# Three of 313 row gathers replaced by single-row copies on SyncE through a table in DRAM

## The chip, the cores and the metric

The kernel runs on one core of one Trainium2 chip. The metric is the time of one execution on the device in microseconds (us). The engines are called as in the profile: PE (TensorE, matrix products; PEld its weight loads), DVE (VectorE), ACT (ScalarE), POOL (GpSimd) and SP (SyncE, which computes nothing here and issues DMAs in the order of its program).

## The reference

One block of a graph network (PaiNN), a residual sum and a layer norm. There are 1250 nodes with 512 features (384 of a vector part `v`, 128 of a scalar part `s`) and 40000 edges, sorted by target node.

```python
x_j = x[src]                                   # a row of its source node for each edge
v_j, s_j = x_j[:, :384].reshape(E, 128, 3), x_j[:, 384:]
s_j = silu(s_j @ W1 + b1) @ W3 + b3            # depends on the node alone
split = s_j * (rbf(edge_weight) * cutoff @ W2 + b2)
s1, s2, s3 = split[:, :128], split[:, 128:256], split[:, 256:]
v_msg = v_j * s1[:, :, None] + s3[:, :, None] * edge_attr[:, None, :]
x = x + segment_sum(concat([v_msg, s2]), dst)
...                                            # second half: messages that depend on the source node alone
return layernorm(x_in + x)
```

## The kernel before, in words

What depends on a node alone is computed once for each node and written to a table in DRAM, `table1`, with rows of 640 numbers (2560 bytes). In the main loop each edge needs the row of its source node, times factors of its own, summed over the edges of a target.

The edges are cut into 79 chunks of 512 and these into tiles of 128 edges, one edge to a partition. Four chunks make a group, and a batch is four tiles, one of each chunk of the group. There are 80 batches (`NT`), numbered `t`: 76 full ones and four with two or three tiles, 313 tiles in all. The loop is written out, so every engine has a straight list of instructions, in the order in which the code makes them.

In step `t` of the loop:

- `messages(t)`: DVE multiplies the gathered rows by the edge factors `eb` in place (L938 and L940), then makes `hot`, `spread` and `pair`, small tables that say which target an edge has.
- `add_messages(t - 1)`: PE sums the messages of the batch before by target (L974, L980).
- `edge_factors(t + 1)`: PE makes `eb` for the next batch (L928); its last instruction is kept in the name `made`.
- `gather(t + 3)`: POOL fetches the rows of the batch three ahead, one indirect DMA for each tile (L769); the first of a batch also waits for `made`. A batch goes into the next of five rooms of SBUF, three of the tile `more` and two of `nodes`.
- other work at steps given by tables (`first`, `early`, `mid`, `late`, `dve`), which for each block of 128 nodes makes the second half's rows and starts the last products.

SP does the small transfers of that work. `fetch_part` (L1088) brings a block of `x` in four quarters into `node_x`, one quarter a step, behind `made`; `take_block` on DVE (L1106) reads it one step after the last quarter for the first block, three steps after it for the others. `keep_part` (L1099) copies the sum of `x` and the first half to `resid` in DRAM, also in quarters and behind `made`. `store_begun` (L1405) writes partial products to `spilled`. Each DMA that SP issues waits for the one eight before it on SP, since eight semaphores are used in turn.

Of the kernel before, what the change touches and what calls it, by code (L numbers as in the profile page):

```python
# [11 lines left out]
F32 = mybir.dt.float32  # L12
# [3 lines left out]
I32 = mybir.dt.int32  # L16
# [5 lines left out]
P = 128  # L22
C = 128
V = 3 * C
# [11 lines left out]
CHUNK = 512  # L36
TPC = CHUNK // P
CPG = 4
SHARE = 16
MARGIN = 8  # L40
# [10 lines left out]
GROUP = 4  # L51
LEAD = 3
LAG = 2


def by_component(ap):
# [8 lines left out]
def gnn_resnorm(  # L65
# [350 lines left out]
    with tc.If(misses_v == 0):  # L416
        windowed(tc, sh)
# [201 lines left out]
def windowed(tc, sh):  # L619
# [13 lines left out]
    nc = tc.nc  # L633
# [12 lines left out]
    def lanes(g, i, j):  # L646

        c = g * CPG + j
        if c >= NCH:
            return 0  # L650
        n = CHUNK if c < NCH - 1 else last_rows
        return max(0, min(P, n - i * P))


    batches = [(g, i) for g in range(NGR) for i in range(TPC) if lanes(g, i, 0)]
    NT = len(batches)

    def tiles(g, i):
        return [j for j in range(CPG) if lanes(g, i, j)]
# [15 lines left out]
        return max(i for i in range(TPC) if lanes(g, i, j))  # L675

    resid = tc.dram_tile([NP, width], F32, name="resid")
    spilled = tc.dram_tile([(NB + 2) * P, width], F32, name="spilled")
    counts = sh.counts
    by_group = counts.rearrange("s (p h) n -> s h p n", h=2)  # L680
# [2 lines left out]
    with tc.tile_pool(  # L683
        name="msg", bufs=4
# [78 lines left out]
        def gather(t, behind=None):  # L763

            g, i = batches[t]
            rows_t = next(rooms)
            for j in tiles(g, i):
                n = lanes(g, i, j)
                got = nc.gpsimd.indirect_dma_start(  # L769
                    out=rows_t[:n, j, :],  # L770
                    out_offset=None,
                    in_=sh.table1,
                    in_offset=bass.IndirectOffsetOnAxis(
                        ap=sh.src_i[:n, g, i * CPG + j : i * CPG + j + 1], axis=0
                    ),
                )
                if behind is not None and j == 0:
                    tc.add_manual_dep(
                        got.ins, behind.ins.name, sync,
                        reason="so that rows come while PE is ahead of DVE",  # L780
                    )
            clear_rest(t, rows_t, nc.gpsimd)
            rows_of[t] = rows_t


        def make_turns(g, n, part):
# [60 lines left out]
        def clear_rest(t, tile, engine=nc.vector):  # L847
            g, i = batches[t]
            for j in tiles(g, i):
                m = lanes(g, i, j)  # L850
                if m < P:
                    engine.memset(tile[m:, j], 0.0)
# [58 lines left out]
        def new_banks(name, sizes):  # L911

            factor_banks.close()
            banks.push(factor_banks)
            of = factor_banks.enter_context(tc.tile_pool(name=name, bufs=1, space=PSUM))
            return [
                of.tile([P, n, BANK], F32, name=f"{name}_{k}") for k, n in enumerate(sizes)
            ]
# [5 lines left out]
        def edge_factors(t):  # L924
            g, i = batches[t]
            for j in tiles(g, i):
                rows = slice(j * FEAT, j * FEAT + N_RBF + 1 + CARRY)
                made = nc.tensor.matmul(  # L928
                    made_in[t][:, j, : V + CARRY], turned[g][rows, i, :], sh.w2_sb[rows, :],
                    start=True, stop=True,  # L930
                )
            return made

        def messages(t):
            g, i = batches[t]
            msg = rows_of.pop(t)
            for js, n, m in runs(g, i):
                nc.vector.tensor_mul(msg[:m, js, V:], msg[:m, js, V:], factors_of(t, js)[:m, :, C:V])  # L938
            for js, n, m in runs(g, i):
                nc.vector.tensor_mul(  # L940
                    msg[:m, js, :V].rearrange("p t (k c) -> p t k c", k=3),
                    msg[:m, js, :V].rearrange("p t (k c) -> p t k c", k=3),
                    factors_of(t, js)[:m, :, None, :C].to_broadcast([m, n, 3, C]),
                )
            make_hot(t)
            make_spread(t)
            run(amid, t)
            make_pair(t)
            msgs[t] = msg
# [18 lines left out]
        def add_messages(t):  # L968
            g, i = batches[t]
            if i == 0:  # L970
                aggs[g] = ps_sum.tile([P, width], F32, name="agg")
            agg, msg, js = aggs[g], msgs.pop(t), tiles(g, i)
            for j in js:
                nc.tensor.matmul(  # L974
                    agg[j * WIN : (j + 1) * WIN, :], hots[t][:, j, :],
                    msg[:, j, :width], start=(i == 0), stop=False, skip_group_check=True,
                )
            for c in range(3):
                for j in js:
                    nc.tensor.matmul(  # L980
                        agg[j * WIN : (j + 1) * WIN, c * C : (c + 1) * C],
                        spread[t][:, j, c, :], msg[:, j, width:],
                        start=False, stop=(i == last_tile(g, j) and c == 2),
                        skip_group_check=True,
                    )

        def count_links(t):

            g, i = batches[t]
            if i == 0:  # L990
                adjs[g] = all_links
            adj, one, pair, js = adjs[g], onehots.pop(t), pairs.pop(t), tiles(g, i)
            to = adj[:, : PARTS * REACH].rearrange("s (p n) -> s p n", n=REACH)
            if i == 0 and g:
                nc.tensor.matmul(
                    to[:, :, : REACH - GSPAN], ident, passed.pop(g),
                    start=True, stop=False, skip_group_check=True,
                )
            for j in js:
                m = lanes(g, i, j)  # L1000
                at = j * SHARE

                nc.tensor.matmul(  # L1003
                    to[:, :, at : at + WIN], one[:m, j, :],
                    pair[:m, j, :].rearrange("e (p n) -> e p n", n=WIN),
                    start=(i == 0 and j == js[0] and g == 0), stop=(i == last_tile(g, j)),
                    skip_group_check=True,
                )
# [457 lines left out]
        first, early, late, dve, mid, amid = {}, {}, {}, {}, {}, {}  # L1466

        def at(when, step, rank, fn, *args):
            when.setdefault(step, []).append((rank, fn, args))
# [16 lines left out]
        for g in range(1, NGR, 2):  # L1486
            base, n = 4 * g - 4, min(2, NGR - g)
# [169 lines left out]
        def run(when, step):  # L1657
            for _, fn, args in sorted(when.get(step, []), key=lambda task: task[0]):
                fn(*args)
# [63 lines left out]
        at(dve, 4, 9, sh.part_bias, nc.vector, node_x[:, : 2 * C], slice(V, V + 2 * C))  # L1723
        at(dve, 4, 9.1, nc.vector.memset, node_x[:MARGIN, : 2 * C], 0.0)
        ahead = 3
        for t in range(ahead - 1):
            gather(t)
        gather(ahead - 1, edge_factors(0))
        behind = set(amid) - {last + 1 for last in last_step.values()}
        for t in range(max(*first, *early, *late, *dve, *mid) + 1):  # L1730
            if t < NT:
                messages(t)
            if t == NT - 4:
                assert all(len(tiles(*batches[u])) == CPG // 2 for u in range(NT - 3, NT))
                made_in[NT - 3], made_in[NT - 2] = new_banks("halves", [CPG // 2] * 2)
                made_in[NT - 1] = made_in[NT - 3]
            if t == NT - 1:
                out_banks.update(zip(in_factors, new_banks("out", [1] * CPG), strict=True))
            run(first, t)
            if 1 <= t <= NT:  # L1740
                add_messages(t - 1)
                if t not in behind:
                    count_links(t - 1)
            run(early, t)
            if t + 1 < NT - 2:
                made = edge_factors(t + 1)
            if t + 1 in (NT - 3, NT - 2):
                edge_factors(t + 2)
            if t + ahead < NT:
                gather(t + ahead, made if t + ahead < NT - 2 else None)  # L1750
            if t in behind:
                count_links(t - 1)
            run(mid, t)
            run(late, t)
            run(dve, t)
        soon_out = 0, 1, 2
        for k, rows in enumerate((upper, lower)):
            for b in soon_out:
# [80 lines left out]
def _general(ctx, tc, sh):  # L1839
# [170 lines left out]
    def edge_sums(table, sums, begin, finish, add, pool, ps_agg):  # L2010
# [13 lines left out]

        for step in range(NT + LAG):
            t = step
            if t < NT:
# [9 lines left out]
                nc.vector.tensor_scalar(hots[t], lane, slots[:, t, 4:5], None, op0=ALU.is_equal)  # L2037
            t = step - LAG
            if t >= 0:
# [134 lines left out]
```

## Time and profile before

| | |
|---|---|
| time, median of 3 runs | 480.09 us (478.63 to 480.22) |
| profiled execution | 480.96 us |
| its span, first to last instruction | 479.2 us |
| busy PE / DVE / ACT / POOL | 84% / 89% / 78% / 70% |
| gathers of L769 | 313, 304.4 us busy, 104.1 us idle ahead of them |
| main loop, first to last L938 of full batches | 35.7 to 420.5 us, some 5.1 us a batch |
| DMA | 123.29 MB, mean 257 GB/s |

Busy shares are means over the whole span. Sequencer work (SP's DMA issues, register instructions, waits) is not counted as busy and has rows of its own, with names that end in q. "Idle before" is time in which an engine stood still ahead of an instruction, and the releaser named is what ended it; "issue" means that nothing in the profile was waited for.

### The profile page before, as it was taken

The numbers are of one execution on the slowest core, as the hardware profiler recorded it, in microseconds if no ns is written. First come the engines' busy times: TensorE is split into PE (matmuls) and PEld (weight loads), VectorE is DVE, ScalarE is ACT, GpSimd is POOL, SyncE is SP. The second block draws the span as 40 slices with busy tenths as digits, with TensorE's granted clock in tenths as the row PEclk, the third lists the DMA queues.
The fourth block names the chain that finished last, engine by engine and source line by source line (L and its number), as shares of the span: only waits on it lengthen the run. The fifth ranks groups of instructions, "written<-read, shape, count | busy, mean of one in ns | idle before, by whom it ended". The sixth has DMA issues, their size and how long they took to land. (4 is left out here: it accounts for less than half of the span.)

```text
span 479.2 us, 11259 instructions
## 1 busy us (share of the span) xinstructions
PE 402.6 (84%) x4259; PEld 229.3 (48%) x4259; DVE 427.8 (89%) x675; ACT 375.3 (78%) x971; POOL 334.9 (70%) x364
## 2 busy tenths in 40 slices
PE   8645586878879778798889888989999999999992
PEld 6322243445445345444435544555555655555782
DVE  6569899999999899999999999999999999978584
ACT  4377846689869968877977897799899889967672
POOL 9267777777777777777777777777777777771530
PEclk9857979899999999989989999999999999999998
DMA  8887888788888888888888988888888888879024
GB/s 238 301 247 253 254 265 271 240 279 262 281 254 272 289 259 275 270 269 255 280 276 255 293 267 280 266 291 287 287 275 293 265 284 291 280 242 319 4 71 151
DMA packets 37810, 123.29 MB, mean 257 GB/s; under 512 B 7124, under 2 KB 9782, under 8 KB 37746
## 3 DMA queue, kind: packets, MB, share of 16 engines
q0 software_dynamic: 25568, 104.34, 69.0%
q1 hardware_dynamic: 10834, 17.35, 10.6%
q10 hardware_dynamic: 1344, 0.79, 0.5%
q8 instruction: 35, 0.57, 0.5%
q14 instruction: 29, 0.24, 0.2%
HBM read 112.94 MB, written 9.51 MB: 256 GB/s over the span
## 5 line engine op out<-in xcount | busy, mean ns | idle before, releaser
L769 POOL DMA_INDIRECT more<-table,src_i x189 | 184.6, 977 | 66.3 <-issue 48.1
L769 POOL DMA_INDIRECT nodes<-table,src_i x124 | 119.8, 966 | 37.8 <-issue 33.2
L903 ACT ACTIVATE one<-one,weight,src_f 128x128 f16<-128x128 f16 x313 | 128.5, 482 | 0.2
L928 PE MATMUL eb<-w_sb,basis_t 25*128 25x388 f32 x614 | 74.1, 551 | 54.3 <-DVE spread L881 43.9
L893 ACT ACTIVATE one<-number,low 128x128 f16<-128x128 f16 x313 | 99.8, 392 | 11.2 <-PE adj L1003 11.2
L940 DVE TENSOR_TENSOR more<-more,eb 128x1536 f32<-128x1536 f32 (+2 forms) x48 | 81.8, 1705 | 0.0
L938 DVE TENSOR_TENSOR more<-more,eb 128x1024 f32<-128x1024 f32 (+2 forms) x48 | 57.0, 1190 | 15.0 <-PE eb L928 8.2
L928 PEld LDWEIGHTS eb<-w_sb,basis_t 25*128 25x128 f32 x614 | 24.7, 187 | 76.5 <-DVE spread L881 63.7
L974 PE MATMUL agg<-more,hot 128*32 128x512 f32 x378 | 52.8, 624 | 0.0
L940 DVE TENSOR_TENSOR nodes<-nodes,eb 128x1536 f32<-128x1536 f32 x30 | 52.4, 1747 | 0.0
L980 PEld LDWEIGHTS agg<-more,spread 128*32 128x32 f32 x1134 | 33.5, 111 | 30.2 <-issue 29.6
L938 DVE TENSOR_TENSOR nodes<-nodes,eb 128x1024 f32<-128x1024 f32 x30 | 36.5, 1216 | 6.9 <-PE eb L928 4.0
L881 DVE TENSOR_TENSOR spread<-hot,eb 128x384 f32<-128x384 f32 (+1 forms) x74 | 40.4, 547 | 2.5
L980 PE MATMUL agg<-more,spread 128*32 128x128 f32 x1134 | 40.2, 273 | 0.0
L958 DVE TENSOR_TENSOR pair<-number,column 128x640 f16<-128x640 f16 (+1 forms) x81 | 38.5, 476 | 0.0
L1003 PE MATMUL adj<-pair,one 128*128 128x160 f16 x313 | 35.4, 235 | 0.3 <-DVE basis L827 0.3
L974 PE MATMUL agg<-nodes,hot 128*32 128x512 f32 x248 | 34.9, 619 | 0.0
L980 PEld LDWEIGHTS agg<-nodes,spread 128*32 128x32 f32 x744 | 22.7, 112 | 20.0 <-issue 19.6
L1003 PEld LDWEIGHTS <-one 128*128 128x128 f16 x313 | 21.6, 100 | 16.0 <-issue 13.5
L845 ACT COPY basis_t<-work 128x512 f32<-128x512 f32 x20 | 11.6, 580 | 22.5 <-PE work L840 22.5
L1378 PE MATMUL begun<-upper,cast 128*128 128x512 f32 x57 | 27.8, 487 | 0.0
L980 PE MATMUL agg<-nodes,spread 128*32 128x128 f32 x744 | 27.5, 277 | 0.0
(299 smaller groups left out, 697.3 us busy)
## 6 DMA issues: line engine op xcount, KB each, us to landing
table<-more SPq DMA_DIRECT2D x10, 320.0 KB
more<-table,src_i POOLq DMA_INDIRECT x189, 4.2
spilled<-begun SPq DMA_DIRECT2D x10, 256.0 KB
more<-spilled SPq DMA_DIRECT2D x2, 1280.0 KB
node_x<-in_x_dram SPq DMA_DIRECT2D x35, 64.0 KB
nodes<-table,src_i POOLq DMA_INDIRECT x124, 4.2
out_dram<-more SPq DMA_DIRECT2D x7, 256.0 KB
nodes<-in_x_dram POOLq DMA_DIRECT2D x2, 768.0 KB
```

What stands on the lines that cost most here:

```text
L769: got = nc.gpsimd.indirect_dma_start(out=rows_t[:n, j, :], out_offset=None, in_=sh.table1, in_offset=bass.IndirectOffsetOnAxis(ap=sh.src_i ...
L881: nc.vector.tensor_mul(spread[t][:m, js], hots[t][:m, js, None, :].to_broadcast(shape), carried(t, js, m)[:, :, :3, None].to_broadcast(shape),
L893: nc.scalar.activation(onehots[t][:, j, :], number[:, :P], AF.Abs, bias=low[:, e : e + 1])
L903: nc.scalar.activation(one, one, AF.Relu, scale=less[:, e : e + 1], bias=worth[:, e : e + 1])
L928: made = nc.tensor.matmul(made_in[t][:, j, : V + CARRY], turned[g][rows, i, :], sh.w2_sb[rows, :], start=True, stop=True,)
L938: nc.vector.tensor_mul(msg[:m, js, V:], msg[:m, js, V:], factors_of(t, js)[:m, :, C:V])
L940: nc.vector.tensor_mul(msg[:m, js, :V].rearrange("p t (k c) -> p t k c", k=3), msg[:m, js, :V].rearrange("p t (k c) -> p t k c", k=3), fac ...
L958: nc.vector.tensor_tensor(pair[:m, js, :].rearrange("p t (l h) -> p t l h", h=2), number[:m, : PARTS * WIN].rearrange("p (l h) -> p l h", ...
L974: nc.tensor.matmul(agg[j * WIN : (j + 1) * WIN, :], hots[t][:, j, :], msg[:, j, :width], start=(i == 0), stop=False, skip_group_check=True,)
L980: nc.tensor.matmul(agg[j * WIN : (j + 1) * WIN, c * C : (c + 1) * C], spread[t][:, j, c, :], msg[:, j, width:], start=False, stop=(i == la ...
L1003: nc.tensor.matmul(to[:, :, at : at + WIN], one[:m, j, :], pair[:m, j, :].rearrange("e (p n) -> e p n", n=WIN), start=(i == 0 and j == js[ ...
L1378: nc.tensor.matmul(acc, casts[a, b], rows[:, a, :], start=(start and a == first and k == 0), stop=(stop and a == end - 1 and k == 1),)
```

## The change

One of the four tiles of the batches 23, 47 and 71 (every 24th full batch, the tile of the last chunk) is no longer gathered. `stage_sources` copies the node numbers of its 128 edges to DRAM before the loop. In 16 portions of eight rows, spread over the steps `t - 23` to `t - 6`, `stage_rows` has SP load node numbers into registers, 16 at a time, and issue one DMA for each edge, from the node's row of `table1` to the edge's row of `stage`, both in DRAM; the row's address comes from the register. In `gather`, three steps ahead of use, one plain DMA of SP brings the 128 rows to the tile's place. All else is as before.

```diff
+STAGE_EVERY = 24
+ROWS_AT_ONCE = 16
...
+    full_batches = [t for t in range(NT) if all(lanes(*batches[t], j) == P for j in range(CPG))]
+    staged = {t: k for k, t in enumerate(full_batches[STAGE_EVERY - 1 :: STAGE_EVERY])}
+    stage = tc.dram_tile([len(staged) * P, V + 2 * C], F32, name="stage")
+    stage_src = tc.dram_tile([len(staged), P], I32, name="stage_src")
...
             for j in tiles(g, i):
                 n = lanes(g, i, j)
+                if t in staged and j == CPG - 1:
+                    continue
                 got = nc.gpsimd.indirect_dma_start(
...
+            if t in staged:
+                k = staged[t]
+                nc.sync.dma_start(rows_t[:, CPG - 1, :], stage[k * P : (k + 1) * P, :])
             clear_rest(t, rows_t, nc.gpsimd)
             rows_of[t] = rows_t
+
+        def stage_sources(t):
+            g, i = batches[t]
+            edge = (g * CPG + CPG - 1) * CHUNK + i * P
+            nc.sync.dma_start(
+                stage_src[staged[t] : staged[t] + 1, :],
+                sh.src[edge : edge + P].rearrange("(o e) -> o e", o=1),
+            )
+
+        def stage_rows(t, first, n):
+            k = staged[t]
+            if first % ROWS_AT_ONCE == 0:
+                _, at_stage[t] = nc.values_load_multi_w_load_instructions(
+                    stage_src[k : k + 1, first : first + ROWS_AT_ONCE],
+                    engines=(mybir.EngineType.SP,), min_val=0, max_val=sh.n_nodes - 1,
+                    skip_runtime_bounds_check_because="nodes of edges lie in the features",
+                )
+            for r in range(first, first + n):
+                nc.sync.dma_start(
+                    stage[k * P + r : k * P + r + 1, :],
+                    sh.table1[bass.ds(at_stage[t][r % ROWS_AT_ONCE] + MARGIN, 1), :],
+                )
...
         ahead = 3
+        to_stage, at_stage = {}, {}
+        for u in staged:
+            stage_sources(u)
+            n = 8
+            for k in range(P // n):
+                to_stage.setdefault(u - STAGE_EVERY + 1 + k * 19 // 16, []).append((u, k * n, n))
...
             run(dve, t)
+            for task in to_stage.get(t, ()):
+                stage_rows(*task)
```

The instruction lists show it at three places. Lines of the changed kernel are numbered anew (L1088, L1099, L1405 and L769 are now L1121, L1132, L1438 and L777; the new ones are L792, L799, L807 and L813). First, SP at the start of the loop, before:

```order
L1719 DMA node_x<-in_L_gnn_bu_dram 3x128 x2
L1088 DMA node_x<-in_x_dram 16x512
L1088 DMA node_x<-in_x_dram 8x512
L1088 DMA node_x<-in_x_dram 32x512 x7
L1099 DMA resid<-h_t 32x512 x4
```

and now, with what each instruction waits for (DMAHW is one of SP's eight semaphores; `ISA` is the register instruction that makes an address):

```order
L1752 DMA node_x<-in_L_gnn_bu_dram 3x128 [waits DMAHW6_49]
L1752 DMA node_x<-in_L_gnn_bu_dram 3x128 [waits DMAHW7_49]
L799 DMA stage_src<-in_src_dram 16x8 [waits DMAHW0_49]
L799 DMA stage_src<-in_src_dram 16x8 [waits DMAHW1_49]
L799 DMA stage_src<-in_src_dram 16x8 [waits DMAHW2_49]
L807 TENSOR_LOAD stage_src [waits DMAHW0_49]
L813 ISA
L813 DMA stage<-table_170 16x40 [waits DMAHW3_49]
```

Between the constants and the first quarter of `node_x` now stand the node numbers' copies and 40 rows, each a register instruction and a DMA that is cut in 16 pieces of 40 numbers.

Second, SP around batch 23, before (the third node block's quarters and the second block's copies to `resid`):

```order
L1088 DMA node_x<-in_x_dram 32x512 [waits DMAHW5_49,DVE_49,PE_49]
L1088 DMA node_x<-in_x_dram 32x512 [waits DMAHW6_49,PE_49]
L1088 DMA node_x<-in_x_dram 32x512 [waits DMAHW7_49,PE_49]
L1088 DMA node_x<-in_x_dram 32x512 [waits DMAHW0_49,PE_49]
L1099 DMA resid<-h_t 32x512 [waits DMAHW1_49,PE_49]
L1099 DMA resid<-h_t 32x512 [waits DMAHW2_49]
L1099 DMA resid<-h_t 32x512 [waits DMAHW3_49,PE_49]
L1099 DMA resid<-h_t 32x512 [waits DMAHW4_49]
```

and now:

```order
L813 DMA stage<-table_170 16x40 [waits DMAHW7_49]
L1121 DMA node_x<-in_x_dram 32x512 [waits DMAHW0_49,DVE_49,PE_49]
L792 DMA nodes<-stage 128x640 [waits DMAHW4_49,DMAHW3_49,DMAHW5_49,DMAHW2_49,DMAHW6_49,DMAHW1_49,DMAHW7_49,DMASW1_49,DMASW0_49]
L1121 DMA node_x<-in_x_dram 32x512 [waits PE_49] x3
L1132 DMA resid<-h_t 32x512 [waits PE_49]
L1132 DMA resid<-h_t 32x512
L1132 DMA resid<-h_t 32x512 [waits PE_49]
L1132 DMA resid<-h_t 32x512 [waits DMAHW0_49]
L807 TENSOR_LOAD stage_src [waits DMAHW1_49]
L813 ISA
```

The load of the staged tile (L792) waits for all rows of it, and the next tile's rows begin behind the four copies to `resid`, which wait for PE.

Third, POOL at the gathers of batch 23, before:

```order
L769 DMA nodes<-table_170,src_i 128x640 [waits DMASW2_49,DVE_49,PE_49]
L769 DMA nodes<-table_170,src_i 128x640 [waits DMASW3_49]
L769 DMA nodes<-table_170,src_i 128x640 [waits DMASW4_49]
L769 DMA nodes<-table_170,src_i 128x640 [waits DMASW5_49]
L769 DMA nodes<-table_170,src_i 128x640 [waits DMASW6_49,DVE_49,PE_49]
```

and now:

```order
L777 DMA nodes<-table_170,src_i 128x640 [waits DMASW2_49,DVE_49,PE_49]
L777 DMA nodes<-table_170,src_i 128x640 [waits DMASW3_49]
L777 DMA nodes<-table_170,src_i 128x640 [waits DMASW4_49]
L777 DMA nodes<-table_170,src_i 128x640 [waits DMASW5_49,DVE_49,PE_49]
L777 DMA nodes<-table_170,src_i 128x640 [waits DMASW6_49]
```

The batch's fourth gather is gone, and the fourth row is now the first gather of batch 24.

## The prediction

> **What bounds the kernel now.** I read the waits of DVE and POOL first, then the busy time by stretches, then SP's own rows. The waits (engine, line, releaser: us in total, times, longest):
>
> ```profile
> POOL more L769 <- issue: 48.1, 158, 0.3
> POOL nodes L769 <- issue: 33.2, 109, 0.3
> DVE more L938 <- PE eb L928: 8.2, 12, 2.7
> DVE more L938 <- DMA more<-table,src_i: 4.1, 5, 1.4
> DVE nodes L938 <- DMA nodes<-table,src_i: 1.1, 1, 1.1
> ```
>
> POOL waits for nothing but its own issue, 0.30 us ahead of each gather, while DVE waits only six times for gathered rows, 5.2 us in all. The stretches (length, then PE, PEld, DVE, ACT, POOL busy with counts, clock, DMA share, GB/s) show why:
>
> ```profile
> 180.00:220.00 40.00, 34.27 (x404) 18.57 (x400) 38.01 (x55) 33.08 (x89) 30.64 (x31) 0.96 0.85 268
> 340.00:380.00 40.00, 38.97 (x433) 21.90 (x432) 38.60 (x57) 36.22 (x95) 30.45 (x32) 1.00 0.88 284
> ```
>
> POOL's 32 gathers with 0.30 us between them fill 40 us: 32 x (0.95 + 0.30) = 40.0. DVE is busy 38.0 to 38.6 of the same 40. So POOL sets the pace by a hair, DVE stands right behind, and a batch takes 5 us on both. The batches that matter here begin with these DVE rows (start, length, and in brackets the idle time and its releaser):
>
> ```profile
> 153.87 1.21 DVE L938 TENSOR_TENSOR nodes<-nodes,eb 128x1024 f32<-128x1024 f32 x1
> 164.97 1.22 DVE L938 TENSOR_TENSOR more<-more,eb 128x1024 f32<-128x1024 f32 x1 [1.43 <-DMA more<-table,src_i]
> 277.81 1.22 DVE L938 TENSOR_TENSOR more<-more,eb 128x1024 f32<-128x1024 f32 x1 [0.38 <-DMA more<-table,src_i]
> 288.83 1.22 DVE L938 TENSOR_TENSOR nodes<-nodes,eb 128x1024 f32<-128x1024 f32 x1 [1.12 <-DMA nodes<-table,src_i]
> 400.44 1.21 DVE L938 TENSOR_TENSOR more<-more,eb 128x1024 f32<-128x1024 f32 x1
> ```
>
> Batches 23, 47 and 71 start at 153.87, 277.81 and 400.44. Those are the deadlines of the three staged tiles.
>
> **What it removes.** Three gathers, 3 x 1.25 = 3.75 us of POOL. Of this DVE can cash only its own waits for gathers. After batch 23 POOL is 1.25 us further ahead: the wait of 1.43 shrinks to 0.18, and later batches and later gathers both move up by 1.25, so their waits stay. After batch 47 another 1.25 us removes the 1.12. After batch 71 no wait for gathers is left to remove. Gain: 1.25 + 1.12 = 2.4 us.
>
> **What it adds on SP.** Per staged tile 128 pairs of a register instruction (`ISA`) and a row DMA, eight loads of 16 registers, and one load of the tile. Nearest rows of SP (first the timeline: start, length; then two lines' own views: ns min/median/max):
>
> ```profile
> 25.23 1.40 SPq L400 DMA_DIRECT2D w_sb<-in_L_gnn_W_dram  x4
> 26.68 0.60 SPq L401 DMA_DIRECT2D w_sb<-in_L_gnn_b_dram  x1
> 27.32 0.44 SPq L153 DMA_DIRECT2D u_sb<-in_L_gnn_U_dram  x1
> 32.46 1.49 SPq L1719 DMA_DIRECT2D node_x<-in_L_gnn_bu_dram  x2
> ...
> L415 SPq TENSOR_LOAD <-missed_i x1: 485/485/485, 31.5 to 31.5; - x1
> L415 SPq FUSED_REGOPS  x1: 192/192/192, 32.0 to 32.0; - x1
> ...
> L1088 SPq DMA_DIRECT2D node_x<-in_x_dram x37: 309/311/382, 67.3 to 400.1; - x37
> ```
>
> The register instruction: L415's has three register operations, and so has each row's (+8, x640, x4). 0.19, with the 0.04 us to the next instruction (26.68 + 0.60 to 27.32) 0.23 us.
>
> The row DMA: between 0.31 (plain loads, L1088) and 0.77 (L1719, 1.49 + 0.04 over 2). The plain ones, L400 among them at (26.68 - 25.23) / 4 = 0.36 with the gap, carry a mark in the built program that L401, L1719 and all 384 row DMAs lack. L401 stands in an unbroken run of DMAs, as the rows will: I take its 0.60 + 0.04 = 0.64. A row is then 0.87 us, 128 rows 111.4.
>
> The load of 16 registers: L415 shows one register from SBUF in 0.485. Lower end 0.485, if 16 come as one. Upper end: 0.192 as the part paid once (the register instruction, which reads no memory) and 0.293 for each register, 4.88. The row is near neither, so I take the middle, 2.68, with the gap 2.72; eight are 21.8. Nothing in the trace reads registers from DRAM, and the upper end could be passed there.
>
> The Trainium skill, Runtime: NRT & Kernel Launch, "Instruction fetch mechanics", gives about 200 ns for each register of such a load even in bulk: 3.2 us for 16 is an estimate by that page, and the sum below would be 593 instead of 581. No run here shows a load of more than one register; its 485 ns fit the page as little as they contradict it.
>
> So a staged tile holds SP for T = 111.4 + 21.8 = 133.2 us, against some 124 us from one deadline to the next.
>
> **What is queued around it on SP.** SP takes its instructions in order, and the old transfers stand between the rows. Today SP mostly waits, and its transfers start when PE and DVE let them:
>
> ```profile
> SPq L1088 <- PE eb L928: 159.1, 35, 6.1
> SPq L1088 <- DVE h_t L1116: 65.5, 8, 11.4
> ...
> 158.59 5.90 SPq L1099 DMA_DIRECT2D resid<-h_t  x4
> ...
> 287.74 0.34 SPq L1405 DMA_DIRECT2D spilled<-begun  x1
> ...
> DMA to landing us min/median/max: 3.8/4.2/5.8
> ```
>
> The last row is that of the gathers, nearest for what a transfer of SP takes to land: 4.2 us. Tile by tile:
>
> Tile 1 can begin once SP is past L1719 (33.95) and the node numbers have landed: 38.2. Then T; 14 old transfers in between, x 0.36 = 5.0; the load of the tile waits for the last rows, 4.2, and lands 4.2 later: 38.2 + 133.2 + 5.0 + 8.4 = 184.8, where DVE wants it at 153.87. Stall 30.9.
>
> Tile 2 stands behind the four L1099, which wait for PE of batches 23 and 24 and end 164.49 - 153.87 = 10.6 after batch 23 starts. 10.6 + 133.2 + 18 x 0.36 + 8.4 = 158.7, against 277.81 - 153.87 = 123.94. Stall 34.8.
>
> Tile 3 stands behind L1405, which ends 288.08 - 277.81 = 10.3 after batch 47 starts. 10.3 + 133.2 + 5.0 + 8.4 = 156.9, against 122.63. Stall 34.3.
>
> Inside these stretches the old transfers are late too: the last quarter of the first node block stands behind 56 rows, four loads and four transfers, 38.2 + 48.7 + 10.9 + 1.4 + 4.2 = 103.4, where DVE first reads it at 87.3:
>
> ```profile
> L1106 DVE TENSOR_TENSOR x<-node_x,work x9: 664/674/700, 87.3 to 414.3; 128x384 f32<-128x384 f32 x9
> ```
>
> DVE thus stops there for 16 us. This is part of the 30.9 and not added to it, since SP is not held up by it. The spills and the copies to `resid` leave late in the same way, also inside the stalls. The gain of 2.4 us goes: where SP sets the start of batches 23, 47 and 71, POOL has been ahead for long.
>
> **DMA engines.**
>
> ```profile
> q0 software_dynamic: 25568, 104.34, 69.0%
> q1 hardware_dynamic: 10834, 17.35, 10.6%
> q10 hardware_dynamic: 1344, 0.79, 0.5%
> ```
>
> Each row is cut in 16 pieces of 160 bytes: 6144 pieces and at most as many closing packets. A packet costs 28 ns (q10: 0.5% x 16 x 479.2 us / 1344) to 75 (q1): 21 to 58 us on each of 16 engines, less 3/313 of 69%. At a share of 0.85 this delays landings somewhat. I put it at nothing, as 4.2 us of landing is covered by the 7 us in which eight rows issue (each row DMA waits for the eighth before it); what is left uncovered, two landings a tile, is in the range.
>
> **Sum.** 30.9 + 34.8 + 34.3 = 100.0 on the profiled execution's 480.96 us (span 479.2; the median of the runs, 480.09, is 0.2% lower): 581 us. In short, time = 481 + 3T - 300, as long as T is above about 102.
>
> **Rivals.**
> *SP keeps up* (the other side). One mechanism: a row with its share of the register loads issues fast enough. Stalls vanish at T = 98 to 102, 0.77 us a row all in, and the first node block is on time at 0.7. With plain DMAs of 0.31 it would be: 128 x 0.58 + 21.8 = 96. Then the gain stands, 478.6 us. Against it: L401, L1719 and the register instruction. 0.16; landings behind fuller DMA engines may eat 2.4 us, so 0.07 for faster, 0.09 for no change.
> *Register loads come as one*, 0.485: T = 111.4 + 8 x 0.525 = 115.6, 481 + 47 = 528. With rows a little cheaper too this reaches down to 490. For it: one instruction; against: 16 registers have to be written. 0.16.
> *Registers come one by one*: T = 111.4 + 8 x 4.92 = 150.8, 634 us. 0.10.
> *Landing paces the rows*: beyond 7 us of landing the wait for the eighth before decides; at 10 us T is 160 + 21.8, 727 us. The gathers' longest is 5.8. 0.02.
>
> **How the numbers follow.** My forecast, each tile late by a fifth to a good third of the 124 us, 550 to 620 us in all, has the remaining 0.56. The range for 8 in 10 takes in the cheap loads and most of the dear ones: 488 to 640. Half a per cent is about what a measurement of this kernel can tell from no change. Faster 0.07, same 0.09, slower 0.84.
>
> **What would show it.** Right: DVE waits of tens of us ahead of L938 at batches 23, 47 and 71, released by the DMA from `stage`, and waits for `node_x` at L1106; SP rows back to back at 0.87 us a pair; register loads of 2 to 4 us; POOL now waiting for PE. Wrong, if the row DMA takes 0.31 or the pair runs under 0.7, if SP idles between rows, or if DVE stops for `node_x` alone; and if row DMAs wait for their eighth predecessor, the landing was the price and not the issue.

## The result, and the profile after

The changed kernel takes 533.76 us (median of 4 runs, 530.62 to 534.63) against 479.51 us before (median of 4, 478.63 to 480.22): ratio 1.112, 95% interval 1.107 to 1.117, 54 us more. The profiled execution took 534.63 us, its span 532.7 against 479.2. Lines of the changed kernel have the new numbers: L777 gathers, L961 makes `eb`, L971 and L973 multiply, L1121 is `fetch_part`, L1132 `keep_part`, L1438 `store_begun`, L1139 reads `node_x`, L1149 writes `h_t`, L792 loads the staged tile, L807 the registers, L813 copies a row.

First the same two stretches as in the prediction, busy time by engine (PE, PEld, DVE, ACT, POOL), clock, DMA share and GB/s, of the changed kernel:

```profile
180.00:220.00 40.00, 33.10 (x407) 18.67 (x408) 38.39 (x56) 34.31 (x93) 30.40 (x32) 0.99 0.87 268
340.00:380.00 40.00, 30.54 (x313) 16.50 (x314) 29.21 (x42) 29.46 (x75) 23.61 (x25) 0.91 0.73 228
```

In the first the loop runs as before (32 gathers, DVE 38.4 of 40), although SP copies the second tile's rows all through it. In the second, 7 gathers and 9 us of DVE are missing: the loss sits in single stops. The waits, as before (us in total, times, longest):

```profile
POOL nodes L777 <- PE eb L961: 33.0, 11, 8.7
POOL more L777 <- PE eb L961: 31.9, 10, 10.0
DVE more L971 <- PE eb L961: 21.1, 15, 8.9
DVE x L1139 <- DMA node_x<-in_x_dram: 20.1, 4, 8.1
DVE h_t L1149 <- DMA resid<-h_t: 18.9, 3, 9.6
ACT begun L1430 <- DMA spilled<-begun: 16.1, 3, 8.8
```

POOL, which before waited for little but its own issue, waits for PE, which waits for DVE. DVE stops for `node_x` to arrive (20.1 us) and for copies of `h_t` to `resid` to be done before it may overwrite `h_t` (18.9 us). ACT waits for the store of the last tile `begun` to `spilled`, and through PE's `eb` this reaches DVE. All three are old transfers of SP. DVE's longest stops and the starts of batches 23, 47 and 71, from its timeline (start, length, line; in brackets the idle time and its releaser):

```profile
93.66 0.66 DVE L1139 TENSOR_TENSOR x<-node_x,work 128x384 f32<-128x384 f32 x1 [8.11 <-DMA node_x<-in_x_dram]
...
146.75 0.69 DVE L1149 TENSOR_TENSOR h_t<-x,node_x 128x512 f32<-128x512 f32 x1 [7.08 <-DMA resid<-h_t]
...
168.66 1.21 DVE L971 TENSOR_TENSOR nodes<-nodes,eb 128x1024 f32<-128x1024 f32 x1
...
288.88 0.69 DVE L1149 TENSOR_TENSOR h_t<-x,node_x 128x512 f32<-128x512 f32 x1 [9.63 <-DMA resid<-h_t]
...
310.79 1.22 DVE L971 TENSOR_TENSOR more<-more,eb 128x1024 f32<-128x1024 f32 x1 [0.45 <-PE eb L961]
...
370.58 1.22 DVE L971 TENSOR_TENSOR more<-more,eb 128x1024 f32<-128x1024 f32 x1 [8.92 <-PE eb L961]
...
453.08 1.22 DVE L971 TENSOR_TENSOR more<-more,eb 128x1024 f32<-128x1024 f32 x1 [1.74 <-DMA more<-stage]
```

Batch 23 starts at 168.66, 14.8 us later than before, and batch 47 at 310.79, 33.0 us later, both without any wait for the staged tile. Only batch 71 (453.08, 52.6 us later) waits for one, 1.74 us. The stop of 8.92 us at 370.58 goes back to a spill, by this chain over SP, ACT and PE:

```profile
362.00 0.37 SPq L1438 DMA_DIRECT2D spilled<-begun  x1
...
366.53 0.59 ACT L1430 COPY begun<-begun 128x512 f32<-128x512 f32 x1 [8.76 <-DMA spilled<-begun]
...
367.69 0.79 PE L1411 MATMUL begun<-upper,cast 128*128 128x512 f32 x1 [7.24 <-ACT cast L1402]
...
368.84 1.68 PE L961 MATMUL eb<-w_sb,basis_t 25*128 25x388 f32 x8
```

Then SP's prices (ns min/median/max, first and last start):

```profile
L813 SPq FUSED_REGOPS  x384: 46/46/51, 38.6 to 443.8; - x192
L813 SPq MOVE stage<-table x384: 29/29/43, 38.7 to 443.9; - x192
L813 SPq DMA_DIRECT2D stage<-table x384: 492/492/1744, 38.7 to 443.9; - x192
...
L807 SPq TENSOR_LOAD <-stage_src x24: 1816/2574/4031, 35.7 to 431.0; - x24
...
L1121 SPq DMA_DIRECT2D node_x<-in_x_dram x37: 310/513/890, 72.4 to 449.1; - x37
```

And SP's own timeline around the first stop, where the last quarter of `node_x` (89.89) stands behind rows and, between 81.0 and 84.5, a register load:

```profile
72.41 0.93 SPq L1121 DMA_DIRECT2D node_x<-in_x_dram  x2
73.56 6.38 SPq L813 DMA_DIRECT2D stage<-table  x8
80.06 0.98 SPq L1121 DMA_DIRECT2D node_x<-in_x_dram  x2
84.48 5.32 SPq L813 DMA_DIRECT2D stage<-table  x8
89.89 0.52 SPq L1121 DMA_DIRECT2D node_x<-in_x_dram  x1
90.61 3.24 SPq L813 DMA_DIRECT2D stage<-table  x5
```

DVE is released at 93.66, 3.8 us after the issue at 89.89. DVE had stood there since 85.55 (93.66 - 8.11).

### The profile page after: what moved, and what is told of

It is laid out like the page before. It is cut to its first block, busy times and chain, and to the rows that moved or that the text cites. A ratio compares the mean times of both kernels' runs of the same rounds, so it can differ in the third digit from the quotient of the medians.

```text
span 532.7 us, 12441 instructions
## 1 busy us (share of the span) xinstructions
PE 422.0 (79%) x4259; PEld 238.4 (45%) x4259; DVE 428.7 (80%) x675; ACT 375.2 (70%) x971; POOL 329.4 (62%) x361
## 5 line engine op out<-in xcount | busy, mean ns | idle before, releaser
L777 POOL DMA_INDIRECT more<-table,src_i x187 | 180.1, 963 | 93.2 <-issue 46.0
L777 POOL DMA_INDIRECT nodes<-table,src_i x123 | 118.9, 966 | 71.7 <-PE eb L961 33.0
L961 PE MATMUL eb<-w_sb,basis_t 25*128 25x388 f32 x614 | 80.1, 593 | 72.3 <-DVE spread L914 60.6
L973 DVE TENSOR_TENSOR more<-more,eb 128x1536 f32<-128x1536 f32 (+2 forms) x48 | 81.7, 1704 | 0.0
L971 DVE TENSOR_TENSOR more<-more,eb 128x1024 f32<-128x1024 f32 (+2 forms) x48 | 56.9, 1188 | 27.7 <-PE eb L961 21.1
L961 PEld LDWEIGHTS eb<-w_sb,basis_t 25*128 25x128 f32 x614 | 26.1, 199 | 94.2 <-DVE spread L914 77.6
L1007 PE MATMUL agg<-more,hot 128*32 128x512 f32 x378 | 56.9, 669 | 0.0
L973 DVE TENSOR_TENSOR nodes<-nodes,eb 128x1536 f32<-128x1536 f32 x30 | 52.4, 1746 | 0.0
L1013 PEld LDWEIGHTS agg<-more,spread 128*32 128x32 f32 x1134 | 35.3, 116 | 33.8 <-issue 32.9
L1013 PE MATMUL agg<-more,spread 128*32 128x128 f32 x1134 | 42.2, 282 | 0.0
L971 DVE TENSOR_TENSOR nodes<-nodes,eb 128x1024 f32<-128x1024 f32 x30 | 36.5, 1217 | 6.7 <-PE eb L961 4.8
L991 DVE TENSOR_TENSOR pair<-number,column 128x640 f16<-128x640 f16 (+1 forms) x81 | 38.4, 475 | 0.0
L1007 PE MATMUL agg<-nodes,hot 128*32 128x512 f32 x248 | 37.6, 663 | 0.0
L1036 PE MATMUL adj<-pair,one 128*128 128x160 f16 x313 | 37.4, 244 | 0.0
L1411 PE MATMUL begun<-upper,cast 128*128 128x512 f32 x57 | 29.4, 515 | 7.2 <-ACT cast L1402 7.2
L1013 PE MATMUL agg<-nodes,spread 128*32 128x128 f32 x744 | 28.9, 288 | 0.0
```

What stands on the lines that cost most here:

```text
L777: got = nc.gpsimd.indirect_dma_start(out=rows_t[:n, j, :], out_offset=None, in_=sh.table1, in_offset=bass.IndirectOffsetOnAxis(ap=sh.src_i ...
L961: made = nc.tensor.matmul(made_in[t][:, j, : V + CARRY], turned[g][rows, i, :], sh.w2_sb[rows, :], start=True, stop=True,)
L973: nc.vector.tensor_mul(msg[:m, js, :V].rearrange("p t (k c) -> p t k c", k=3), msg[:m, js, :V].rearrange("p t (k c) -> p t k c", k=3), fac ...
L991: nc.vector.tensor_tensor(pair[:m, js, :].rearrange("p t (l h) -> p t l h", h=2), number[:m, : PARTS * WIN].rearrange("p (l h) -> p l h", ...
L1007: nc.tensor.matmul(agg[j * WIN : (j + 1) * WIN, :], hots[t][:, j, :], msg[:, j, :width], start=(i == 0), stop=False, skip_group_check=True,)
L1013: nc.tensor.matmul(agg[j * WIN : (j + 1) * WIN, c * C : (c + 1) * C], spread[t][:, j, c, :], msg[:, j, width:], start=False, stop=(i == la ...
```

## The experiments

Theory A: SP takes its instructions in order and has too little time, so the old small transfers wait behind row copies, and DVE, ACT and PE wait for those. Rival B, the prediction's place: the staged tile is late for its batch. Rival C: the traffic of the row copies slows other transfers.

The kernels of one lot ran on one chip, beside the kernel before. In two lots that took 478.9 and 478.7 us, as in the result. In the other two it took 561.1 and 567.1 us; those come last, since something else bounds the loop there.

**Rows beside the gathers.** The `continue` and the load of the staged tile are taken out:

```diff
-                if t in staged and j == CPG - 1:
-                    continue
...
-            if t in staged:
-                k = staged[t]
-                nc.sync.dma_start(rows_t[:, CPG - 1, :], stage[k * P : (k + 1) * P, :])
```

> The same kernel as e1_rows_beside (rows and register loads stay, all 313 gathers too, no load of a staged tile), where the kernel before takes 479 us again and not 561. Theory A (old transfers behind the rows): 525 to 536 us. Rival B (the staged tile is late): 479 to 486 us. Rival C (traffic of the row copies): 525 us or more too; the next run but one parts it from A.

Measured: 530.39 us, ratio 1.109 (1.103 to 1.115). Nobody reads the table, and the time stays: B falls as the cause of these 52 us (530.39 against 478.85). DVE stops for the same transfers as in the changed kernel:

```profile
DVE h_t L1144 <- DMA resid<-h_t: 18.4, 3, 9.5
ACT begun L1425 <- DMA spilled<-begun: 15.6, 2, 8.2
DVE x L1134 <- DMA node_x<-in_x_dram: 14.8, 3, 8.1
```

**Old transfers on ACT's queue.** In `fetch_part`, `keep_part` and `store_begun`:

```diff
-            after_factors(nc.sync.dma_start(
+            after_factors(nc.scalar.dma_start(
...
-            nc.sync.dma_start(spilled[n * P : (n + 1) * P, :], to)
+            nc.scalar.dma_start(spilled[n * P : (n + 1) * P, :], to)
```

> The same kernel as e3_old_on_act (rows on SP, old transfers issued by ACT). Theory A: old transfers on time, at most the first staged tile some 4 us late: 479 to 492 us. Rival C (traffic): 525 us or more. In the run where the kernel before took 561 us this kernel was no better than the one with the old transfers behind the rows, which speaks for C there.

Measured: 505.11 us (498.49 to 507.36), ratio 1.051 (1.044 to 1.059). A miss: half of the loss goes, half stays. The waits of the profiled execution (507.36 us) say what stayed:

```profile
DVE more L971 <- DMA more<-stage: 13.8, 2, 9.2
DVE nodes L971 <- DMA nodes<-stage: 9.8, 1, 9.8
```

And those of SP's queue:

```profile
SPq L813 <- DMA node_x<-in_x_dram: 18.7, 9, 4.5
SPq L813 <- DMA spilled<-begun: 8.6, 5, 3.2
```

The waits for `node_x` and `resid` are gone from DVE's list. In their place the three staged tiles are late, 9.8 + 13.8 = 23.6 us of the 28.5 us that this execution is longer than the kernel before, at the place that the prediction named. What ACT loses on the issues that it takes over was not tried alone; by this count it has at most the 4.9 us that are left. SP needed 119.8 us from the first register load (35.5) to the load of the first tile (155.3), 132.4 and 129.4 us from one tile's load to the next, against 124 and 123 between the deadlines. The expectation for the same kernel in another lot (e3, below) had 111 us: it left out that the rows wait for transfers of the other queue, 27.3 us in SP's two lines. B is thus real, and in the changed kernel it was hidden: the old transfers delayed DVE so much that the tile was there in time.

**Two tiles, evenly spread.**

```diff
-STAGE_EVERY = 24
+STAGE_EVERY = 36
...
-            n = 8
+            n = 4
...
-                to_stage.setdefault(u - STAGE_EVERY + 1 + k * 19 // 16, []).append((u, k * n, n))
+                to_stage.setdefault(u - STAGE_EVERY + 1 + k, []).append((u, k * n, n))
```

> Two staged tiles instead of three (every 36th batch: 35 and 71), and their rows in 32 portions of four, one a step, instead of 16 of eight in 19 steps: SP has 4 x 0.69 + 2.7 / 4 = 3.4 us of rows in a step of 5.1. Theory A: an old transfer waits for four rows and at most a register load, 5.4 us, so nearly all are on time: 477 to 485 us. Rival C (two thirds of the traffic): about 515 us. Rival D (any staged tile costs a fixed stall at its use): 479 + 2 x 18 = 515 us.

Measured: 477.29 us (12 runs), ratio 0.998 (0.995 to 1.000): no loss, and no gain that can be told from none. By C, and by D (a fixed stall at each staged tile), it would be about 515 us: neither is seen. A row costs as much as in the changed kernel (median 0.492 us for the copy), but SP again has time to wait for PE, 58.9 us ahead of L1121, where it has 13.8 in the changed kernel and 159.1 before:

```profile
SPq L1121 <- PE eb L961: 58.9, 22, 6.5
```

**Rows from fixed addresses.** No registers, no register loads, all 384 row copies in place, from every fifth node and not from the nodes that the edges name:

```diff
-            if first % ROWS_AT_ONCE == 0:
+            if False:
...
-                    sh.table1[bass.ds(at_stage[t][r % ROWS_AT_ONCE] + MARGIN, 1), :],
+                    sh.table1[5 * r + MARGIN : 5 * r + MARGIN + 1, :],
```

> The same kernel as f5_static_rows, for a chip on which the kernel before takes 479 us: 384 row copies from fixed addresses (wrong rows), no registers, no register loads, old transfers on SP. Its rows took 0.632 us each on SP where the kernel before took 567 us. With that a tile takes 128 x 0.632 = 81 us and with the old transfers some 90, within the 97 us of its 19 steps. Theory A (SP's time is the price): 477 to 484 us. Rival C (the traffic of 384 row copies, all of which is still there): 505 us or more.

Measured: 479.69 us (10 runs), ratio 1.002 (0.999 to 1.004). C falls for these chips: the traffic of all 384 rows is there and costs nothing measurable. What went is SP's time:

```profile
L813 SPq DMA_DIRECT2D stage<-table x384: 467/587/1744, 32.7 to 378.8; - x192
```

A row is 0.587 us and 0.045 to the next: 0.632 instead of 0.685 us, so a tile holds SP for 81 us. In the changed kernel it is 128 x 0.685 + 8 x 2.61 (the load's median and the gap) = 108.6 us; 20.9 of the 27.6 us between them are the register loads.

**The gathers' part alone.** Three gathers replaced by plain loads of neighbouring rows, no row copies:

```diff
-                nc.sync.dma_start(rows_t[:, CPG - 1, :], stage[k * P : (k + 1) * P, :])
+                nc.sync.dma_start(rows_t[:, CPG - 1, :], sh.table1[MARGIN : MARGIN + P, :])
...
-            for task in to_stage.get(t, ()):
-                stage_rows(*task)
```

> The same kernel as e2_no_rows (three gathers replaced by plain loads of 128 neighbouring rows, no row copies). The prediction's gain of 2.4 us: 477 us against 479.5. If DVE's own work is the bound, 479 to 480.

Measured: 479.04 us (12 runs) against 478.85 (23 runs), ratio 1.002 (0.999 to 1.004). The gain of 2.4 us is not there; the interval leaves at most 0.6 us. In the profiled execution DVE waits for gathered rows no shorter than before (for `more` 5.8 us against 4.1, for `nodes` 0.9 against 1.1), and at other batches:

```profile
DVE more L971 <- DMA more<-table,src_i: 5.8, 5, 1.6
```

One of them, from DVE's timeline:

```profile
316.95 1.22 DVE L971 TENSOR_TENSOR more<-more,eb 128x1024 f32<-128x1024 f32 x1 [1.25 <-DMA more<-table,src_i]
```

This wait of 1.25 us lies behind two saved gathers. DVE and POOL need nearly the same time for a batch, and where the one has to wait for the other differs between the two executions; the waits of one execution are no sum that saved gathers cash.

**The lots in which the kernel before took 561 and 567 us.** Here the same kernels, and two more: the 16 registers loaded once for a tile, so that all its 128 rows come from 16 nodes,

```diff
-            if first % ROWS_AT_ONCE == 0:
+            if first == 0:
```

with the old transfers on SP (e4, f4) and on ACT (f8).

> All register loads and row copies of SP stay as in the changed kernel, but nobody reads the table: all 313 gathers stay and the three loads of staged tiles are gone. Theory A (the old small transfers of SP wait behind the rows in SP's order, and DVE, PE and ACT wait for those): the time stays, 525 to 536 us. Rival B (the staged tile comes too late for its batch, as predicted): the delay goes with the load, 479 to 486 us.

> The three gathers are gone, and their tiles come by one plain load of 128 rows in a row from the table of nodes (other nodes than the edges name, so this leaves out the right rows); no register loads, no row copies. This is what the change could gain at most. The prediction's 2.4 us of gather waits would give 477 us against 479.5; if POOL's lead is not worth anything, 479 to 480.

> Rows, register loads and staged tiles as in the changed kernel, but the old transfers of the loop (quarters of node_x, copies to resid, spills) are issued by ACT's queue. Theory A: the old transfers are on time again. SP then needs about 111 us for a tile, so the first staged tile lands at about 38 + 111 + 8 = 157, some 4 us late, the others on time: 481 to 492 us with what ACT loses on 81 issues. Rival C (the row copies' 6144 small pieces and their traffic slow the DMA engines for all): nothing changes, 525 us or more.

> The 16 registers are loaded once for a tile and used for all its 128 rows (so the table gets wrong nodes from row 16 on): 21 of 24 register loads are gone, 56 us of SP in all, 18.6 a tile; the traffic of the rows stays. Theory A: a tile holds SP for 128 x 0.69 + 2.7 = 91 us, and with 14 old transfers of 0.5 it just keeps step with its 19 steps of 5.1 us (97 us): 480 to 495 us. Rival C (traffic): 525 to 534 us.

> The same kernel as e4_loads_once (16 registers loaded once for a tile, so 21 of 24 register loads are gone; wrong nodes from row 16 on; old transfers on SP). Theory A: SP needs 128 x 0.685 + 2.7 = 90 us for a tile, with 14 to 18 old transfers of 0.5 about 99, against 19 steps of 5.1 = 97: it just keeps step, old transfers wait for little more than one portion of 5.5 us, 479 to 490 us. If the backlog needs a margin and not only T below the 97, 490 to 515 us.

> The rows come from fixed addresses (every fifth node, so wrong rows), with no register and no register load; 128 row copies a tile and their traffic stay. If the row copy costs SP 0.49 us for being a copy of one row, a tile takes 63 us; if the register in its address makes it dear, 0.31 to 0.36 and 40 to 46 us. Either way SP has room: theory A 477 to 481 us. Rival C (traffic of the small pieces): 525 us or more.

> Old transfers issued by ACT as in f3_old_on_act (505 us, where DVE waited 9.8, 9.2 and 4.6 us for the three staged tiles) and registers loaded once for a tile as in f4_loads_once. Theory A with the predicted deadline as its second half: a tile takes some 100 us instead of 120 to 131, so the three waits for staged tiles go as well: 477 to 483 us. If ACT's 81 issues are what f3 paid for: 495 to 505 us.

| kernel | us | ratio (95%) |
|---|---|---|
| e1 rows beside the gathers | 592.89 | 1.060 (1.054 to 1.066) |
| e2 no rows | 559.78 | 0.997 (0.994 to 1.001) |
| e3 old transfers on ACT | 594.63 | 1.060 (1.054 to 1.067) |
| e4 loads once | 584.83 | 1.041 (1.036 to 1.047) |
| f4 loads once | 593.76 | 1.049 (1.041 to 1.057) |
| f5 fixed addresses | 591.04 | 1.042 (1.032 to 1.051) |
| f8 loads once, old on ACT | 593.56 | 1.045 (1.036 to 1.053) |

The expectations were made for a kernel before of 479 us, and except for the ratio of e2 neither theory's numbers are met as ratios: every kernel with rows is 4 to 6% slower here, the one with old transfers on ACT and the one with few register loads too, and f5, the same kernel that lost nothing above. That SP's work and the queue of the old transfers matter so little here is closer to C than to A, but no run tests C here. The timeline of e2, which has no rows, shows what is different:

```profile
347.53 0.93 PE L961 MATMUL eb<-w_sb,basis_t 25*128 25x388 f32 x8 [0.27 <-issue]
...
349.98 1.22 DVE L971 TENSOR_TENSOR more<-more,eb 128x1024 f32<-128x1024 f32 x1 [1.06 <-PE adj L1036]
```

DVE begins 1.52 us after the end of `eb` (347.53 + 0.93 to 349.98). The bracket names a later PE instruction, `adj`, as the releaser; that DVE waits here for `eb` is inferred. Over all starts of L971 after an idle time above 0.25 us the median of that step is 1.36 us (65 starts), where in f2, the same kernel on the other chip, it is 0.07 us (18 starts). From DVE to PE it is 0.06 us in both. 65 starts with 1.29 us more are 84 us, in size the 82 us between 479 and 561; that this is their whole cause is argued, not shown. Why that step is long there, and why rows then cost 24 to 34 us even with fixed addresses, stays open, so theory A and the fall of C are shown only for chips on which the kernel before takes 479 us.

## Why the prediction was right or wrong

**The sign and the bound: right.** SP, which waited most of the time before, is the bound, since it takes its instructions in order. With less of SP's time (f9), or with fewer rows in more steps (f6), the loss is gone. POOL waits for PE, as said. The place of the loss was wrong, see below.

**The row: mis-sized.** Predicted 0.23 for the register instruction and 0.64 for the copy, 0.87 us. Measured 0.046 + 0.029 + 0.492 and three gaps, 0.685 us. Of the 0.185 us too much, some 0.105 lie in the copy (0.492 with its gap against 0.64) and 0.08 in the register instruction. L401's 0.60 is close to a copy from a fixed address, 0.587 in f9, and not to one from a register. The 0.192 of L415 was a single register instruction; 384 in a stream take a quarter of it each.

**The register load: right in size.** Predicted 2.68, measured 2.574 in the median, from 1.8 to 4.0. The prediction took the middle of two bounds because no row was near, so that it came this close is luck. The rival of one cheap load of 0.485 is out, and that of 4.88 too. The Trainium skill, Runtime: NRT & Kernel Launch, "Instruction fetch mechanics", has about 200 ns for a register; here it is 2.574 / 16 = 0.161 us, and the measurement decides.

**So T was too long.** From the medians it is 128 x 0.685 + 8 x 2.61 = 108.6 us, not 133.2. By the prediction's formula the time would be 481 + 3 x 108.6 - 300 = 507 us. The changed kernel takes 534.

**The step that failed: "part of the 30.9 and not added to it, since SP is not held up by it".** DVE was to stop at batches 23, 47 and 71 for the tile, and late quarters and copies were to be contained in that stop. They are the stops themselves: 20.1 us for `node_x`, 18.9 for `resid`, 8.9 behind a spill, and 1.74 for a staged tile. Ahead of batch 23 there are two long ones, 8.11 + 7.08 = 15.2 us, and the batch starts 14.8 us late, 8.5 us after the load of its tile was issued (160.12). Without any read of a staged tile (f1) the time is the same. And SP is held up, through a ring: a late transfer stops DVE, DVE stops PE, and SP's next old transfer waits for PE. SP's timeline of the changed kernel around batch 23:

```profile
160.12 0.36 SPq L792 DMA_DIRECT2D nodes<-stage  x1
160.53 8.36 SPq L1121 DMA_DIRECT2D node_x<-in_x_dram  x3
173.37 5.51 SPq L1132 DMA_DIRECT2D resid<-h_t  x4
```

Three loads of `node_x` stretch over 8.36 us and four copies to `resid` over 5.51, where each takes about 0.5 us. In between SP waits for PE, and behind batch 47 for DVE's `begun` (the second row), as its waits over the whole span say:

```profile
SPq L1121 <- PE eb L961: 13.8, 6, 5.0
SPq L1438 <- DVE begun L1443: 9.6, 1, 9.6
SPq L1132 <- PE eb L961: 8.4, 2, 4.5
```

The two terms for this wait were right: the first register load of the next tile comes 10.2 and 10.3 us after batches 23 and 47 start (178.9 - 168.66 and 321.1 - 310.79), where the prediction had 10.6 and 10.3. Wrong was what these starts wait for.

The 27 us between 507 and 534 can be told from the trace. From a tile's first register load to the load of the tile SP takes 124.4, 124.8 and 126.7 us (from 35.7, 178.9 and 321.1 to 160.12, 303.72 and 447.78), where 108.6 and the prediction's terms for old transfers and for the last rows' landing make 117.8, 119.3 and 117.8: 21 us more, since an old transfer takes about 0.5 us instead of 0.36, and not every row and load keeps to its median (the longest row copy took 1.744 us). From there to the start of the batch it is 8.5, 7.1 and 5.3 us instead of 4.2, another 8 us, at batches 23 and 47 since DVE is still behind, at 71 since the tile itself comes late. SP's earlier starts, 35.7 instead of 38.2 above all, give 3 us back.

With the old transfers on another queue (f3) the stops for tiles come back at batches 23, 47 and 71. That its 505 us lie near the 507 of the formula is luck: in f3 SP has no old transfers between the rows and no wait of 10 us behind a batch, and its rows wait 27.3 us for the other queue instead. Two errors of opposite sign thus lie in the 581: T costs 3 x 24.6 = 74 us too much, and 27 us are missing. That the time fell inside the range of 488 to 640 owes something to this. Of the prediction's own signs of error, a pair under 0.7 us came true; stops at `node_x` alone came true in part, as DVE stops for `resid` and behind a spill as well.

**The gain: wrong.** 2.4 us were read from single waits of one execution; f2 leaves at most 0.6.

**DMA engines at nothing: right** where the kernel before takes 479 us (f9).

## What to carry to other kernels

A queue that mostly waits is not free: what counts is the time of the new instructions between two old ones against the slack of the old ones, and each old transfer has a deadline of its own, to be listed beside that of the new work. When work is put on such a queue, spread it so that each step's share fits well within the step (3.4 us in each step of 5.1 us, and 81 us in the 97 of 19 steps, cost nothing here; 108.6 in 97 cost 54 us in all), and ask who waits for the old transfers before asking who waits for the new. A gain that rests on a few waits of one profiled execution should be tried alone first.

## What was not expected of the hardware

- A row copy whose address comes from a register takes SP 0.492 us, one with a fixed address 0.587; with its two register instructions the first is still only 0.05 us dearer.
- A register load of 16 numbers from DRAM takes 1.8 to 4.0 us of SP, 0.16 us a number in the median.
- The same plain load of `node_x` takes SP 0.311 us before (median of 37) and 0.513 us among row copies.
- On two lots' chips the step from the end of PE's `eb` to DVE's start took 1.36 us in the median, on the others 0.07 us.
